# A hybrid layer's scans: adding two states' products by a transfer from GpSimd's queue, and the sum on TensorE a unit later

## The chip, the cores and the metric

One core of a Trainium2 chip runs the whole kernel as one program. The metric is the device time of one execution in microseconds. Of the core's engines, TensorE multiplies matrices into PSUM banks; VectorE, ScalarE and GpSimd work elementwise; SyncE's queue issues most of the transfers, and GpSimd can issue transfers from its own queue too. Each engine takes its instructions in the order of its own queue and waits on semaphores for the others.

## What is computed

Four blocks with residual connections run over an input of 4 sequences, 1024 tokens and 128 channels: a sparse attention, an MLP with sign weights, a Mamba block (a selective scan), and the same MLP again. The change touches the Mamba block:

```python
def step(h, inp):
    dt_t, B_t, C_t, u_t = inp
    dA = jnp.exp(dt_t[..., None] * A)
    h = dA * h + (dt_t * u_t)[..., None] * B_t[:, None, :]
    y_t = jnp.einsum('ben,bn->be', h, C_t)
    return (h, y_t)
h0 = jnp.zeros((B, E, N), x.dtype)
...
_, ys = lax.scan(step, h0, xs)
y = ys.transpose(1, 0, 2) + u2 * D_param
y = y * jax.nn.silu(z)
out = jnp.einsum('ble,ed->bld', y, W_out)
return x + res_scale * out
```

There are E = 256 channels and N = 16 states of each channel. The scan runs along the tokens, on its own for each channel and state. `y_t` is the sum over the 16 states of the state times its C.

## The kernel before

**Parts and units.** The attention runs first, up to about 242 us. Then come the first MLP and the Mamba block's preparation, and from about 312 to 866 us the scans, with the MLPs' work set between them. The scans' work is cut into eight parts, one for each of 4 sequences `b` and 2 halves `f` of its tokens (512 columns), and each part into 16 units, one for each state `n`: 128 units. A unit holds all 256 channels as two blocks `h` of 128 partitions, so that a tile `[128, 2, 512]` of float32 (512 KB) is one state of one part.

**One unit i**, by engine:

- GpSimd, `drive`: `db[i]`, the products of `dt * u` and B, one instruction of 128 x 1024, written two units ahead into one of three buffers. B comes, spread over the partitions, by a transfer `bs` of 512 KB for every two units, from SyncE's queue (`load_b`).
- ScalarE, `decay`: `da[i, h]`, the exponentials, one instruction for each block, a unit ahead.
- VectorE: two scans, one for each block, into `hs`; then one product of 128 x 1024 of `hs` with C into `hc[i]` (`hss[i]` in the code, six buffers).
- TensorE: C spread over the partitions into the one PSUM bank `pcc`, from which that product reads; and the sum over the states.

**The sum over the states.** Two states' products are first added on GpSimd (`fold`): the pair k, k + 1 (k even) is added block by block into `hc[k + 1]`, block 0 in unit k + 2 and block 1 in unit k + 3. Then TensorE (`total`) adds the pair's sum to the PSUM bank `pys` of its block, with the identity as its weights: block 0 in unit k + 3 and block 1 in unit k + 4. The first such matmul of a part comes after one with `skip_d`, which is `u2 * D_param`. After a part's last pair VectorE multiplies the gate with `pys` (`gated`), block 0 in unit k + 4 and block 1 in unit k + 5, and `mamba_out` (or `mamba_out_own` for the last four parts) multiplies it with `W_out`.

**What sets the order.** Within the scans each engine's instructions keep the order in which the program issues them. A planner sets the other work (MLP matmuls, evictions, normalisation steps, the next parts' preparation) between them: `pieces` takes pieces of it as long as the engines' clocks in `times` allow, and `spend` moves these clocks by a cost written beside each step, 1.29 for an addition of `fold`. These costs steer the order alone. The last lines of `scans` run the steps that remain after unit 127.

**The end.** After unit 127 the last pair is added and summed, the gate multiplied, and `mamba_out_own(3, 1)` and the last MLP follow in series. In TensorE's queue the rest of another MLP (tiles `pfc`, `pgc`, `pfoc`) stands between these steps.

Of the kernel before, what the change touches and what calls it, by code (L numbers as in the profile page):

```python
# [22 lines left out]
ALU = mybir.AluOpType  # L23
# [20 lines left out]
def hybrid_kernel(ctx: ExitStack, tc: tile.TileContext, x, Wq, Wk, Wv, Wo, ln_g, ln_b, W_in, conv_w,  # L44
# [17 lines left out]
    ve, te, sc, gp = (InOrder(e) for e in (nc.vector, nc.tensor, nc.scalar, nc.gpsimd))  # L62
# [1071 lines left out]
    def scans(wide, ready):  # L1134

        bss, dbs, das, hss = {}, {}, {}, {}
        py = {}
        last = len(units) - 1  # L1140

        def load_b(i):

            if i <= last and i % 2 == 0:
                b, f, n = units[i]
                ready(b, f, "b")
                bss[i] = m2.tile([P, 2, CH], F32, name=f"bs{i}", tag="bs", bufs=2)
                nc.sync.dma_start(bss[i], mamba_pre[b, f][5][n : n + 2, :].partition_broadcast(P))

        def drive(i):  # L1150
            if i <= last:
                b, f, n = units[i]
                ready(b, f, NH - 1)
                dbs[i] = m2.tile([P, NH, CH], F32, name=f"db{i}", tag="db", bufs=3)
                bs = bss[i - n % 2][:, n % 2]
                gp.tensor_tensor(dbs[i], mamba_pre[b, f][3], bs.unsqueeze(1).to_broadcast([P, NH, CH]), ALU.mult)

        def decay(i, h):
            if i <= last:
                b, f, n = units[i]  # L1160
                das[i, h] = wide.tile([P, CH], F32, name=f"da{i}_{h}", tag="da", bufs=2)
                sc.activation(das[i, h], mamba_pre[b, f][2][:, h], AF.Exp, scale=a_t[:, h, n : n + 1])

        def fold(i):

            h = i % 2
            k = i - 2 - h
            if 0 <= k <= last:
                gp.tensor_add(hss[k + 1][:, h], hss[k + 1][:, h], hss[k][:, h])

        def total(i):

            h = 1 - i % 2
            k = i - 3 - h
            if not 0 <= k <= last:
                return
            b, f, n = units[k]
            if n == 0:
                py[b, f, h] = wide.tile([P, CH], F32, name=f"pys{b}_{f}{h}", tag=f"pys{h}")
                te.matmul(py[b, f, h], skip_d[:, h], mamba_pre[b, f][1][:, h], start=True, stop=False)  # L1180
            te.matmul(py[b, f, h], ident, hss[k + 1][:, h], start=False, stop=n == N - 2)

        def gated(i):

            h = i % 2
            k = i - 4 - h
            if not 0 <= k <= last:
                return False
            b, f, n = units[k]
            if n == N - 2:  # L1190
                gate = mamba_pre[b, f][0]
                ve.tensor_mul(gate[:, h], gate[:, h], py.pop((b, f, h)))
                if h == NH - 1:
                    fed.add(("g", b, f))
            return n == N - 2


        done = {}

        def after(*keys):  # L1200
            return [done.get(k, 0.0) for k in keys]

        for i in range(3):
            load_b(i)
        for i in range(2):
            drive(i)
            done["db", i] = spend("gp", 2.38)
        for h in range(NH):
            decay(0, h)
            done["da", 0, h] = spend("sc", 0.7)  # L1210
        for i, (b, f, n) in enumerate(units):
            now[0] = i
            load_b(i + 3)
            fold(i)
            h0, h1 = i % 2, 1 - i % 2
            done["fold", i] = spend("gp", 1.29, *after(("hc", i - 1 - h0)))
            drive(i + 2)
            done["db", i + 2] = spend("gp", 2.38, *after(("hs", i - 1, 1)))
            pc = wide.tile([P, CH], F32, name=f"pcc{i}", tag="pcc")
            te.matmul(pc, spread[: 6 * N, n, :], mamba_pre[b, f][4], start=True, stop=True)  # L1220
            done["pcc", i] = spend("pe", 0.4, *after(("hc", i - 1)))
            hs = m2.tile([P, NH, CH], F32, name=f"hs{i}", tag="hs")
            db = dbs.pop(i)
            for h in range(NH):
                first = carry[b % 2][:, h, n : n + 1] if f else 0.0
                ve.tensor_tensor_scan(hs[:, h], das.pop((i, h)), db[:, h], first, ALU.mult, ALU.add)
                done["hs", i, h] = spend("ve", 1.235 if f else 1.175, *after(("da", i, h), ("db", i)))
            decay(i + 1, 0)
            done["da", i + 1, 0] = spend("sc", 0.67, *after(("hs", i, 0)))

            t = times["ve"]
            pieces(t + 2.5, lumps=False)
            if f == 0:
                sc.copy(carry[b % 2][:, :, n : n + 1], hs[:, :, CH - 1 :])
            decay(i + 1, 1)
            done["da", i + 1, 1] = spend("sc", 0.67 if f else 0.86, *after(("hs", i, 1)))
            if gated(i):
                spend("ve", 0.68, *after(("sum", i - 1)))
            hss[i] = m2.tile([P, NH, CH], F32, name=f"hc{i}", tag="hc", bufs=6)
            ve.tensor_tensor(hss[i], hs, pc.unsqueeze(1).to_broadcast([P, NH, CH]), ALU.mult)  # L1240
            done["hc", i] = spend("ve", 1.205, *after(("pcc", i)))
            total(i)
            done["sum", i] = spend("pe", 1.0, *after(("fold", i - 1)))
            t = times["ve"]
            pieces(t + 2.2)
        for i in range(last + 1, last + 6):
            fold(i)
            gated(i)
            total(i)
# [6 lines left out]
    def spend(engine, us, *others):  # L1256
        times[engine] = max(times[engine], *others, 0.0) + us
        return times[engine]
# [36 lines left out]
    def pieces(until, lumps=True):  # L1295

        forced = not until
        evictions(lumps, forced)  # L1300
        for k, rate in RATES.items():
            owed[k] = min(max(owed[k], -2 * rate) + (0 if forced else rate / 2), rate / 2)
        left = SPARE - sum(w.held for w in works)

        for w in works[:-2] + sorted(works[-2:], key=lambda w: w.count):

            moved = w in emptied and now[0] < len(units) - 10
            while w.may() and not w.next.evict and w.next.banks <= left:
                if moved and not w.next.same and not (forced and w in emptied):
                    break  # L1310
                if not (forced or w.next.hurries()):
                    if any(us and owed[k] <= 0 for k, us in w.next.us.items()):
                        break
                    if "pe" in w.next.us and ends(w)[0]["pe"] > until:
                        break
                left -= w.next.banks
                issue(w)
                moved = True
            if forced and moved:
                break  # L1320

    def ready(*part):
        while part not in prepared:
            pieces(None)
# [50 lines left out]
    with banks(SPARE), tc.tile_pool(name="wide", bufs=1, space=PSUM) as wide:  # L1375
# [21 lines left out]
        ])  # L1397
        among_scans[0] = True
        scans(wide, ready)
        among_scans[0] = False  # L1400
        works.insert(0, Work(mamba_out_own(B - 1, 1)))
# [40 lines left out]
```

## Time and profile before

| | us |
|---|---|
| median of 3 runs | 905.94 (905.73 to 910.06) |
| span of the profiled execution, first to last instruction | 901.9 |
| TensorE busy, of the span | 756.2 (84%) |
| VectorE busy | 754.3 (84%) |
| GpSimd busy | 727.0 (81%) |
| ScalarE busy | 607.1 (67%) |

The span is measured on the chip by the profiler in one execution, and the times in the first row come from runs of their own. The profile's page lists groups of instructions: engine, operation, output <- inputs, shape, count, then busy time, the mean of one in ns, the idle time just before them and what ended it. Nearly all rows name line 57, since a helper there issues every instruction; the tiles' names tell them apart. `PEld` is TensorE's loading of weights, `PE` its matmuls. A wait is put down to what came last. A row of waits reads: engine and tile, what ended the wait, us in total, times, the longest. A row of the timeline reads: start, length, engine, line, operation, tiles, shape, and in brackets the idle time before it. A table of stretches reads: from:to, length, busy us (and instructions) of each engine, the granted share of TensorE's clock, the busy share of the 16 DMA engines, and GB/s.

Two more rows for the scans, ScalarE's exponentials and VectorE's scan from a carried state:

```profile
L57 ACT ACTIVATE da<-dt,a_t 128x512 f32<-128x512 f32 x256 | 175.5, 688 | 123.2 <-DVE hs L57 122.7
L57 DVE TENSOR_TENSOR_SCAN hs<-da,carry,db 128x512 f32<-128x512 f32 x128 | 156.9, 1266 | 1.2 <-ACT da L57 1.2
```

### The profile page before, as it was taken

The numbers are of one execution on the slowest core, as the hardware profiler recorded it, in microseconds if no ns is written. First come the engines' busy times: TensorE is split into PE (matmuls) and PEld (weight loads), VectorE is DVE, ScalarE is ACT, GpSimd is POOL, SyncE is SP. The second block draws the span as 40 slices with busy tenths as digits, with TensorE's granted clock in tenths as the row PEclk, the third lists the DMA queues.
The fourth block names the chain that finished last, engine by engine and source line by source line (L and its number), as shares of the span: only waits on it lengthen the run. The fifth ranks groups of instructions, "written<-read, shape, count | busy, mean of one in ns | idle before, by whom it ended". The sixth has DMA issues, their size and how long they took to land. (4 is left out here: it accounts for less than half of the span.)

```text
span 901.9 us, 16464 instructions
## 1 busy us (share of the span) xinstructions
PE 756.2 (84%) x6226; PEld 463.5 (51%) x6226; DVE 754.3 (84%) x994; ACT 607.1 (67%) x1358; POOL 727.0 (81%) x566
## 2 busy tenths in 40 slices
PE   5897779866798978879899888779889989989777
PEld 2454546544577642335456554335455545656457
DVE  6799999999533289798899999989988898999962
ACT  4776648744445488888787888888777766654423
POOL 6799958998322199999999999999988987997930
PEclk9899989987789997789999999899989999999899
DMA  4733123330100111121221211212111121221100
GB/s 127 131 73 70 43 44 69 72 65 2 43 7 1 49 53 66 67 74 48 70 69 51 70 48 70 72 47 72 70 72 59 53 78 59 70 82 58 60 7 19
DMA packets 47152, 53.18 MB, mean 59 GB/s; under 512 B 4808, under 2 KB 38384, under 8 KB 47072
## 3 DMA queue, kind: packets, MB, share of 16 engines
q1 hardware_dynamic: 45904, 51.59, 20.4%
q8 instruction: 49, 0.80, 0.4%
q0 software_dynamic: 608, 0.27, 0.2%
q10 hardware_dynamic: 560, 0.26, 0.1%
q14 instruction: 31, 0.25, 0.1%
HBM read 45.82 MB, written 4.46 MB: 56 GB/s over the span
## 5 line engine op out<-in xcount | busy, mean ns | idle before, releaser
L57 POOL TENSOR_TENSOR db<-du,bs 128x1024 f32<-128x1024 f32 x128 | 302.4, 2363 | 0.1
L57 ACT ACTIVATE da<-dt,a_t 128x512 f32<-128x512 f32 x256 | 175.5, 688 | 123.2 <-DVE hs L57 122.7
L57 POOL TENSOR_TENSOR hc<-hc,hc 128x512 f32<-128x512 f32 x128 | 162.8, 1272 | 29.1 <-DVE hc L57 28.8
L57 DVE TENSOR_TENSOR hc<-hs,pcc 128x1024 f32<-128x1024 f32 x128 | 155.9, 1218 | 23.7 <-PE pcc L57 15.4
L57 DVE TENSOR_TENSOR_SCAN hs<-da,db 128x512 f32<-128x512 f32 x128 | 149.4, 1207 | 20.7 <-ACT da L57 15.5
L57 DVE TENSOR_TENSOR_SCAN hs<-da,carry,db 128x512 f32<-128x512 f32 x128 | 156.9, 1266 | 1.2 <-ACT da L57 1.2
L57 PE MATMUL pys<-hc,ident 128*128 128x512 f32 x256 | 145.3, 651 | 6.1 <-POOL hc L57 6.0
L57 POOL TENSOR_TENSOR prodv<-vS,E 128x128 f32<-128x128 f32 (+14 forms) x30 | 69.3, 2311 | 11.5 <-ACT E L57 11.3
L57 PEld LDWEIGHTS pys<-hc,ident 128*128 128x128 f32 x256 | 49.8, 208 | 53.7 <-issue 28.1
L57 PE MATMUL pcc<-bc,spread 96*128 96x512 bf16 x128 | 51.5, 402 | 29.6 <-DVE hc L57 28.7
L57 PE MATMUL pga<-h1a,w 128*128 128x512 f32 x256 | 70.5, 425 | 2.7 <-DVE h1a L57 1.9
L57 POOL TENSOR_TENSOR prod<-kv,qs 128x128 f32<-128x128 f32 (+14 forms) x30 | 71.1, 2369 | 0.8 <-DVE or L57 0.8
L57 ACT ACT_TABLE_LOAD x48 | 61.6, 1283 | 3.5 <-issue 2.6
L57 PE MATMUL pc<-mxnT,w_conv 128*128 128x512 f32 x128 | 61.5, 606 | 2.0 <-ACT gate L57 2.0
L57 PEld LDWEIGHTS pga<-h1a,w 128*128 128x128 f32 x256 | 49.3, 195 | 25.5 <-issue 4.7
L57 ACT ACTIVATE E<-S 128x512 f32<-128x512 f32 (+15 forms) x62 | 26.5, 473 | 39.7 <-DVE S L57 39.5
L57 PE MATMUL ps<-kx,qT 64*32 64x256 f32 x1008 | 43.5, 416 | 5.8 <-DVE S L57 5.0
L57 POOL TENSOR_TENSOR du<-dt,u 128x512 f32<-128x512 f32 x16 | 20.4, 1275 | 30.5 <-ACT dt L57 30.5
L57 ACT COPY ep<-pt 128x512 f32<-128x512 f32 x32 | 18.7, 586 | 35.8 <-DVE eo L57 35.5
L57 PEld LDWEIGHTS pc<-mxnT,w_conv 128*128 128x128 f32 x128 | 24.6, 194 | 33.9 <-issue 26.7
L57 PE MATMUL pgb<-h1b,w 128*128 128x512 f32 x128 | 37.5, 439 | 4.8 <-DVE h1b L57 3.3
L57 PE MATMUL pgc<-h1c,w 128*128 128x256 f32 (+1 forms) x192 | 37.2, 346 | 0.0
(244 smaller groups left out, 1637.5 us busy)
## 6 DMA issues: line engine op xcount, KB each, us to landing
bs<-bd SPq DMA_DIRECT2D x64, 512.0 KB
vr<-vd SPq DMA_DIRECT2D x32, 256.0 KB
vd<-kv SPq DMA_DIRECT2D x8, 256.0 KB
x<-in_L_attn_a_x_dram SPq DMA_DIRECT2D x15, 128.0 KB
kx<-kT SPq DMA_DIRECT2D x104, 16.0 KB
out_dram<-x SPq DMA_DIRECT2D x8, 128.0 KB
taps<-in_L_attn_b_conv_w_dram SPq DMA_DIRECT2D x1, 512.0 KB
out_dram<-ox SPq DMA_DIRECT2D x2, 256.0 KB
```

Source lines behind the costliest of these rows:

```text
L57: ins = getattr(self.engine, name)(*args, **kwargs)
```

## The change

`fold` no longer adds on GpSimd. For each pair GpSimd issues one transfer in SBUF that adds `hc[k]` (both blocks, 512 KB) into `hc[k + 1]`, in unit k + 2, behind that unit's `drive` where the additions stood ahead of it. `total` sums block 0 in unit k + 4 and block 1 in unit k + 5, and `gated` follows in units k + 5 and k + 6: both one unit later than before. The planner is told 0.9 for a transfer in place of 1.29 for each addition, and a sum on TensorE that depends on the transfer of two units before. The loop after the last unit is one longer.

```diff
--- before.py
+++ after.py
@@ -1163,15 +1163,16 @@
 
         def fold(i):
 
+            k = i - 2
+            if k % 2 or not 0 <= k <= last:
+                return False
+            gp.dma_start(hss[k + 1], hss[k], accum_op=ALU.add)
+            return True
+
+        def total(i):
+
             h = i % 2
-            k = i - 2 - h
-            if 0 <= k <= last:
-                gp.tensor_add(hss[k + 1][:, h], hss[k + 1][:, h], hss[k][:, h])
-
-        def total(i):
-
-            h = 1 - i % 2
-            k = i - 3 - h
+            k = i - 4 - h
             if not 0 <= k <= last:
                 return
             b, f, n = units[k]
@@ -1182,8 +1183,8 @@
 
         def gated(i):
 
-            h = i % 2
-            k = i - 4 - h
+            h = 1 - i % 2
+            k = i - 5 - h
             if not 0 <= k <= last:
                 return False
             b, f, n = units[k]
@@ -1211,11 +1212,10 @@
         for i, (b, f, n) in enumerate(units):
             now[0] = i
             load_b(i + 3)
-            fold(i)
-            h0, h1 = i % 2, 1 - i % 2
-            done["fold", i] = spend("gp", 1.29, *after(("hc", i - 1 - h0)))
             drive(i + 2)
             done["db", i + 2] = spend("gp", 2.38, *after(("hs", i - 1, 1)))
+            if fold(i):
+                done["fold", i] = spend("gp", 0.9, *after(("hc", i - 1)))
             pc = wide.tile([P, CH], F32, name=f"pcc{i}", tag="pcc")
             te.matmul(pc, spread[: 6 * N, n, :], mamba_pre[b, f][4], start=True, stop=True)
             done["pcc", i] = spend("pe", 0.4, *after(("hc", i - 1)))
@@ -1240,10 +1240,10 @@
             ve.tensor_tensor(hss[i], hs, pc.unsqueeze(1).to_broadcast([P, NH, CH]), ALU.mult)
             done["hc", i] = spend("ve", 1.205, *after(("pcc", i)))
             total(i)
-            done["sum", i] = spend("pe", 1.0, *after(("fold", i - 1)))
+            done["sum", i] = spend("pe", 1.0, *after(("fold", i - 2)))
             t = times["ve"]
             pieces(t + 2.2)
-        for i in range(last + 1, last + 6):
+        for i in range(last + 1, last + 7):
             fold(i)
             gated(i)
             total(i)
```

In the built program GpSimd's queue has 64 transfers in place of 128 additions. Its other instructions, and those of the other engines, are the same in number up to the grouping, but the planner sets them in another order. In TensorE's queue the last pair's sums now stand ahead of eight `pgc` and four `pfc` matmuls that stood ahead of them before.

## The prediction

> **What bounds the kernel now.** First the table of stretches, to see which engine is full in the stage that the change touches. It runs from the first `du` product (312 us) to the end of the last product with C (866.45); then comes the end of the program, which runs in series.
>
> ```profile
> core 0: us, PE busy (x) PEld busy (x) DVE busy (x) ACT busy (x) POOL busy (x), PEclk, DMA share, GB/s
> 312.00:866.45 554.45, 478.19 (x1731) 269.17 (x1730) 504.58 (x493) 414.49 (x876) 514.04 (x381) 0.92 0.19 64
> 866.45:869.80 3.35, 1.87 (x4) 0.78 (x5) 0.69 (x1) 0.00 (x0) 2.48 (x2) 1.00 0.00 0
> 869.80:884.05 14.25, 13.02 (x101) 10.91 (x99) 4.41 (x16) 3.98 (x11) 1.26 (x2) 1.00 0.04 10
> ```
>
> GpSimd is busy for 93% of the stage, VectorE for 91%, TensorE for 86%: 554.45 / 128 = 4.33 us a unit. Then the groups, for what one instruction costs:
>
> ```profile
> L57 POOL TENSOR_TENSOR db<-du,bs 128x1024 f32<-128x1024 f32 x128 | 302.4, 2363 | 0.1
> L57 POOL TENSOR_TENSOR hc<-hc,hc 128x512 f32<-128x512 f32 x128 | 162.8, 1272 | 29.1 <-DVE hc L57 28.8
> L57 DVE TENSOR_TENSOR hc<-hs,pcc 128x1024 f32<-128x1024 f32 x128 | 155.9, 1218 | 23.7 <-PE pcc L57 15.4
> ```
>
> A high share is not yet a bound: GpSimd runs ahead over three `db` buffers and itself waits 28.8 us for VectorE. So I asked who ended VectorE's waits in the scans, and what TensorE did before them:
>
> ```profile
> DVE hc L57 <- PE pcc L57: 15.4, 16, 2.9
> DVE hs L57 <- ACT da L57: 8.4, 14, 1.5
> ...
> DVE hs L57 <- POOL db L57: 3.0, 3, 1.6
> DVE hs L57 <- POOL hc L57: 2.1, 1, 2.1
> ```
>
> ```profile
> 360.35 0.50 PEld L57 LDWEIGHTS pys<-hc,ident 128*128 128x128 f32 x2 [1.50 <-POOL hc L57]
> ...
> 363.07 0.63 PE L57 MATMUL pcc<-bc,spread 96*128 96x512 bf16 x1
> ...
> 363.74 1.22 DVE L57 TENSOR_TENSOR hc<-hs,pcc 128x1024 f32<-128x1024 f32 x1 [1.85 <-PE pcc L57]
> ```
>
> VectorE waits for `db` for 3.0 us in all. Behind the 2.1 us put down to `hc`, ScalarE's `da` had ended only 0.1 us earlier, so I don't count it. The second fence shows the other path: TensorE's queue stands at a sum because the addition is late, so the spread C comes late and VectorE waits 1.85 us. VectorE, with other engines' small delays, sets the pace; GpSimd rarely does.
>
> **The change, part by part.**
>
> *GpSimd.* 128 additions of 1.272 us go (162.8); 64 issues come. The nearest rows are its own issues at the start:
>
> ```profile
> 247.71 0.70 POOL L869 DMA_DIRECT2D dp<-in_L_attn_b_D_param_dram  x1
> 248.40 2.12 POOL L880 DMA_DIRECT2D w_xp<-in_L_attn_b_W_xp_dram  x3
> ```
>
> ```profile
> kx<-kT POOLq DMA_DIRECT2D x8, 16.0 KB, 6.0
> w_xp<-in_L_attn_b_W_xp_dram POOLq DMA_DIRECT2D x3, 32.0 KB, 2.2
> ```
>
> I take 2.12 / 3 = 0.71, as `w_xp` also names 128 partitions; the least such row is 0.54 (`kx`), the most 1.15 (the first of the constants). So 64 x 0.71 = 45, and GpSimd falls to 514 - 163 + 45 = 396 us, 71% (70% to 77%). An issue would have to cost 162.8 / 64 = 2.54 us to give nothing back. Call T the end of the pair's second product. The issue stands behind a `db` that may start when VectorE's scan ends, T - 1.22, and ends at T + 1.14, so it finds its input ready; the `db` and layer-norm steps queued behind it wait for 0.71 us, not for data.
>
> *What VectorE gets of it.* The 3.0 us for `db`, and those `pcc` waits that come within 6 us of a sum held up by the addition: 1.85, 1.01 and 0.51 (at 363.7, 479.5 and 610.4), 3.4 together: 6.4 us. Ends: 0, if other waits take their place, and 15.4 + 3.0 + 2.1 = 20.5, if every wait for `pcc` and GpSimd goes. I take 6.4, the ones that I can follow.
>
> *The landing.* No accumulating transfer is in the trace. Nearest are GpSimd's transfers, 2.2 to 6.0 us from issue to landing, and a `bs` load of the same 512 KB:
>
> ```profile
> 561.00:563.30 2.30, 0.60 (x3) 0.21 (x2) 2.20 (x3) 2.26 (x5) 2.30 (x2) 1.00 0.61 228
> ```
>
> 228 GB/s for 2.30 us is 524 KB, the whole load. I take 2.2 + 2.3 = 4.5 us; ends 2.2 (all of it overlapped) and 6.0 + 2.3 = 8.3. TensorE reaches the sum behind `pcc` of unit k+4, whose bank is freed at T + 2 x 4.33 = T + 8.7; the issue is at T + 1.1, so 7.5 us are hidden. TensorE's idle time, (554 - 478) / 64 = 1.2 us a pair, covers up to 8.7. Cost taken: nothing; at 8.3 TensorE loses 0.8 a pair, inside its idle time. VectorE's new wait, a product written where a transfer still reads, is for a transfer three units old (13 us). The extra 33.5 MB double the DMA share of 0.19 or, with the destination read too, bring it to some 0.6. `bs` has two units, 8.7 us, for its 2.3.
>
> *One unit later.* The six `hc` buffers hold: a pair's second lives for five units, its first until the landing. The gate and what hangs on it come 4.33 us later at each part's end; other pieces fill that, except at the end. The planner, told that GpSimd is lighter, spreads the other work anew. I take nothing; half of the 15.4 us of `pcc` waits, 7 either way, is its bound.
>
> *The end, where nothing covers the landing.*
>
> ```profile
> 865.23 1.22 DVE L57 TENSOR_TENSOR hc<-hs,pcc 128x1024 f32<-128x1024 f32 x1
> ...
> 866.52 2.48 POOL L57 TENSOR_TENSOR hc<-hc,hc 128x512 f32<-128x512 f32 x2 [4.82 <-DVE hc L57]
> ...
> 867.84 2.35 PE L57 MATMUL pys<-hc,ident 128*128 128x512 f32 x4 [1.52 <-POOL hc L57]
> ```
>
> Now the sums end at 867.84 + 2.35 = 870.19. Then: issue 866.52, landed 871.0, two sums of 0.59 us, 872.2: 2.0 later. In the built order eight `pgc` (1.31 us) and four `pfc` (0.71), which stood before the last sums, come behind them: 2.0 more, on a TensorE busy 13.02 of the next 14.25 us. Together +4.0; ends 1.7 and 7.8 (landing 2.2 and 8.3).
>
> *Weighed against the Trainium skill.* DMA: Bandwidth & Descriptors (Anatomy of one DMA) gives a GpSimd transfer about 2.0 us plus bytes at 436 GB/s. By it the landing would be an estimated 3.2 us and the end 1.3 us shorter than by the rows; no run here shows it yet. SBUF — State Buffer (The "DVE blocks DMA" trap) speaks against the change: while VectorE runs a two-port instruction, GpSimd can't write descriptors. If every issue waited out a scan (1.27 us in the rows), 64 issues would take 127 us, still under 162.8, and the end would grow by 1.3; the eight `kx` issues took 0.54 to 0.81 us beside VectorE's products from PSUM, so this trace shows no such stall.
>
> **Sum.** The profiled span is 901.9; the median of the runs, 905.94, is 4.1 more, which I take as what lies around a span. 901.9 - 6.4 + 4.0 = 899.5, plus 4.1: **903.6 us**. 0.5% is 4.5 us, about what can be told from no change here: faster is under 901.4, slower over 910.5. This case's own range is 895 to 911.
>
> **Rivals.**
> - *GpSimd was the pace-setter:* all 20.5 us go: 905.9 - 20.5 + 4.0 = **889.4**. For it: 93% busy, and a `db` that never waits (0.1 us). Against: VectorE waited for `db` three times in 128 units.
> - *Hidden anyway:* the delays from GpSimd turn into waits for ScalarE or TensorE, and only the end is paid: **909.9**, up to 917 if the new order costs 7. For it: most of VectorE's waits name ScalarE or TensorE. Against: the 1.85 us above, where the addition is plainly first.
> - *TensorE is held by the landing (slower):* in TensorE's queue at the sum, in every second unit. It decides from 8.7 us on: each further us is 64. At 9.0 us: 905.9 + 0.3 x 64 + 4.0 + 4.5 (the longer end) = **933.6**. For it: an accumulation also reads its destination, which no row prices, and it meets the `bs` load. Against: both largest rows together make 8.3.
>
> **How the numbers follow.** Forecast 0.38, pace-setter 0.17, hidden anyway 0.25, held by the landing 0.20. Of the forecast 0.15 is faster, 0.21 same, 0.02 slower; the pace-setter is all faster; hidden anyway is 0.10 same and 0.15 slower; the last all slower. Faster 0.32, same 0.31, slower 0.37. The range 888 to 930 leaves out the far half of the last case and the edge of the second, some 0.15.
>
> **What would show it.** Right: GpSimd near 71% and still no wait of VectorE for `db`; issue rows of 0.7 us; the `pys` waits of TensorE for `hc` gone from the stage; the last `pys` some 5.8 us after the last product instead of 3.7. Wrong: `pys` or `pcc` waits that end with the transfer in every second unit; issue rows over 2.5 us; or VectorE over 95% busy in the stage, which would make the pace-setter right.

## The result, and the profile after

| | before | after |
|---|---|---|
| median, us | 906.46 (20 runs) | 911.53 (20 runs, 907.84 to 912.77) |
| ratio after : before | | 1.0047, 95% interval 1.0035 to 1.0060 |
| span of the profiled execution | 901.9 | 908.9 |
| first product's end to last product's end ("the scans") | 544.0 | 544.8 |
| last product's end to the span's end ("the end") | 35.5 | 41.5 |

The changed kernel is slower by 0.47%: within the 0.5% that the prediction calls no change, but the interval lies wholly on the slow side, where a gain was forecast (903.6), and 911.53 is just above the 911 where the case's own range ends. Of the 7.0 us of span 0.7 are in the scans and 6.0 in the end. What was to be won in the scans did not come.

The table of stretches, of the kernel after, with the stage up to the last product's end and then the end:

```profile
core 0: us, PE busy (x) PEld busy (x) DVE busy (x) ACT busy (x) POOL busy (x), PEclk, DMA share, GB/s
312.00:867.43 555.43, 482.07 (x1719) 267.08 (x1718) 504.28 (x493) 413.69 (x873) 416.37 (x318) 0.91 0.50 124
867.43:874.00 6.57, 1.96 (x3) 0.84 (x3) 0.00 (x1) 0.00 (x0) 0.86 (x1) 0.82 0.42 81
874.00:888.00 14.00, 14.00 (x95) 11.63 (x94) 4.64 (x16) 4.47 (x13) 1.26 (x2) 0.84 0.04 11
```

GpSimd fell from 514 to 416 us of the stage (93% to 75%), and the stage kept its length: 555.43 for 554.45. VectorE is as busy as before, 504.28. Now GpSimd's two groups, and the row of the transfers (issues, KB, median landing):

```profile
L57 POOL TENSOR_TENSOR db<-du,bs 128x1024 f32<-128x1024 f32 x128 | 305.3, 2395 | 71.6 <-DVE hs L57 37.7 <-issue 31.6 <-POOL db L57 1.8
L57 POOL DMA_DIRECT2D hc<-hc x64 | 57.7, 902 | 18.7 <-DVE hc L57 18.4
```

```profile
hc<-hc POOLq DMA_DIRECT2D x64, 512.0 KB, 4.6
```

An issue takes 0.90 us and a landing 4.6. Ahead of `db`, where GpSimd never stood idle before (0.1 us), it now does so for 71.6 us in all: GpSimd has room. VectorE's waits from 320 to 872 us show why this room brought nothing:

```profile
DVE hc L57 <- PE pcc L57: 23.6, 17, 3.4
DVE hs L57 <- ACT da L57: 15.6, 12, 8.3
DVE x L57 <- PE pfoa L57: 1.8, 2, 1.3
DVE hs L57 <- POOL rs_fb L57: 1.0, 1, 1.0
```

The waits for `db` and for the additions are gone, and those for TensorE's `pcc` have grown from 15.4 to 23.6 us. (The 8.3 in the second line is the wait of the very first scan, ahead of the first product.) Last, the chain that sets the end, in order of time (start, length, what):

```profile
866.21 1.23 DVE hc L57
867.44 0.29 issue
867.73 4.53 DMA hc<-hc
872.26 0.04 issue
872.31 3.78 PE pys L57 x4
876.09 1.71 PE pgc L57 x8
877.80 0.83 PE pfc L57 x4
```

After the last product the lone landing stands on the path for 4.53 us, and then the last two sums take 3.78 us. Each sum shows as two matmul records, and late in the scans one sum takes 1.02 us, so 3.78 is nearly twice the usual.

### The profile page after: what moved, and what is told of

Its sections match the earlier page's. It is cut to its first block, busy times and chain, and to the rows that moved or that the text cites. A ratio compares the mean times of both kernels' runs of the same rounds, so it can differ in the third digit from the quotient of the medians.

```text
span 908.9 us, 16459 instructions
## 1 busy us (share of the span) xinstructions
PE 762.8 (84%) x6226; PEld 463.4 (51%) x6226; DVE 754.0 (83%) x994; ACT 607.4 (67%) x1358; POOL 627.9 (69%) x502
## 5 line engine op out<-in xcount | busy, mean ns | idle before, releaser
L57 POOL TENSOR_TENSOR db<-du,bs 128x1024 f32<-128x1024 f32 x128 | 305.3, 2395 | 71.6 <-DVE hs L57 37.7
L57 DVE TENSOR_TENSOR hc<-hs,pcc 128x1024 f32<-128x1024 f32 x128 | 156.0, 1219 | 31.7 <-PE pcc L57 23.6
L57 PE MATMUL pys<-hc,ident 128*128 128x512 f32 x256 | 148.0, 664 | 4.6 <-DMA hc<-hc 4.6
L57 POOL DMA_DIRECT2D hc<-hc x64 | 57.7, 902 | 18.7 <-DVE hc L57 18.4
L57 ACT ACTIVATE E<-S 128x512 f32<-128x512 f32 (+15 forms) x62 | 26.5, 472 | 39.6 <-DVE S L57 39.4
```

Of the source, the lines that this page charges most:

```text
L57: ins = getattr(self.engine, name)(*args, **kwargs)
```

## The experiments

All runs, with the kernel before on the same chip beside each. The scans, the end and the waits of VectorE for `pcc` (320 to 872 us) are from one profile of each; where the first unit begins varies by 4 us between profiles whatever the kernel, so the scans are measured from product to product. A few us between two profiles are no finding by themselves: up to the last product the kernel after, D and E are the same program and show 544.8, 541.8 and 541.8, and F and K are the same and show 538.8 and 541.5. A, H and L have 6 runs each, after has 20, the others 12. The runs stand on several chips, so a comparison of two of them goes first by their ratios to before.

| run | median | ratio (interval) | scans | end | `pcc` waits |
|---|---|---|---|---|---|
| before | 906 | 1 | 544.0 | 35.5 | 15.4 |
| after | 911.53 | 1.0047 (1.0035 to 1.0060) | 544.8 | 41.5 | 23.6 |
| A, old order, nothing added | 899.95 | 0.9921 (0.9897 to 0.9946) | 539.4 | 33.8 | 12.4 |
| B, new order, nothing added | 904.59 | 0.9980 (0.9962 to 0.9997) | 543.3 | 34.0 | 21.1 |
| C, new order, GpSimd's additions | 908.70 | 1.0020 (1.0002 to 1.0039) | 544.0 | 38.2 | 21.4 |
| D, after, last pair on TensorE | 904.33 | 0.9984 (0.9965 to 1.0002) | 541.8 | 35.8 | 21.3 |
| E, after, TensorE kept busy at the end | 908.20 | 1.0027 (1.0007 to 1.0046) | 541.8 | 38.9 | 21.3 |
| F, transfer, old unit, old costs | 907.09 | 1.0009 (0.9991 to 1.0027) | 538.8 | 41.4 | 15.2 |
| G, transfer, later unit, old costs | 908.55 | 1.0033 (1.0010 to 1.0056) | 536.0 | 49.7 | 13.5 |
| H, transfer, old unit, new costs | 911.65 | 1.0053 (1.0034 to 1.0072) | 536.6 | 44.5 | 16.0 |
| I, before, last pair on TensorE | 904.66 | 0.9993 (0.9973 to 1.0013) | 544.1 | 35.0 | 15.4 |
| K, F with the last pair on TensorE | 901.95 | 0.9950 (0.9932 to 0.9968) | 541.5 | 35.1 | 15.7 |
| L, K, planner told heavier | 908.82 | 1.0045 (1.0028 to 1.0062) | 549.7 | 34.3 | 23.8 |
| M, K, planner told lighter | 905.42 | 0.9990 (0.9973 to 1.0008) | 538.0 | 39.4 | 16.9 |

### What GpSimd's relief is worth, in the old order and in the new (A, B, C)

A is the kernel before with `fold` left out; the even states are missing from its output.

```diff
             h = i % 2
             k = i - 2 - h
-            if 0 <= k <= last:
-                gp.tensor_add(hss[k + 1][:, h], hss[k + 1][:, h], hss[k][:, h])
+            return
```

> The kernel before without GpSimd's additions: TensorE sums the odd states' products alone, the even states' are left out of the sum. Every engine's order is that of before. It is the ceiling of what taking the additions off GpSimd can bring. Theory (GpSimd's additions hold nobody; VectorE and TensorE's slow stretches set the pace): the scans take the same time within 2 us, and only the end is shorter, by the 1.4 us from the last product to the first sum and some of the second addition: 903 to 905 us beside 906.5. Rival (the relief is worth what the prediction said or more, and the transfers or the new order take it back): the scans are 6.4 to 20 us shorter, 884 to 898 us.

B is the kernel after, in its order, without the transfers (the even states are missing here too):

```diff
-            gp.dma_start(hss[k + 1], hss[k], accum_op=ALU.add)
             return True
```

> The changed kernel's order, instruction for instruction, without the 64 transfers: nothing adds the even states' products, so that they are missing from the output. Theory (the new order itself costs what GpSimd's relief gives): scans of 542 to 544 us although GpSimd has neither additions nor transfers, where the same removal in the old order gave 539.4, and an end about as long as there plus the pgc and pfc behind the sums (33 us): about 905. Rival (the transfers cost the scans 5 us, by traffic, by issue time or by waits, and the order is free): scans of 539 us and about 901.

C is the kernel after, in its order, with GpSimd adding both blocks in one instruction:

```diff
-            gp.dma_start(hss[k + 1], hss[k], accum_op=ALU.add)
+            gp.tensor_add(hss[k + 1], hss[k + 1], hss[k])
```

> The changed kernel with GpSimd's addition (one instruction of 128 x 1024) in the place of each transfer: same order on every engine, same later sum, no transfers. Theory (order and lag cost nothing in the scans, the loss lies at the end where the landing stands alone): scans as before within 2 us, the end some 2.5 us shorter than the changed kernel's and TensorE less slow behind it: 906 to 909 us. Rival (the new order costs what the relief gives): with GpSimd loaded again the scans are 6 us longer or more: 914 us or more.

In the old order, taking all additions away saves 0.8%: some 7 us, of which 1.7 are in the end (35.5 to 33.8) and about 5 in the scans (544.0 to 539.4). That is the most that relief of GpSimd alone can bring there, and it lies between A's two expectations. In the new order it brings little or nothing: the scans take 544.0 us with additions, 541.8 to 544.8 in the three profiles with transfers (after, D, E) and 543.3 with neither. B and A do the same work, and B is 0.9980 - 0.9921 = 0.6%, about 5 us, slower, by its order alone (the later unit and the planner's costs together), as the theory for B had it. VectorE's waits say where. First A, then B, and then C:

```profile
DVE hs L57 <- ACT da L57: 20.4, 17, 8.3
DVE hc L57 <- PE pcc L57: 12.4, 13, 4.3
```

```profile
DVE hc L57 <- PE pcc L57: 21.1, 15, 3.9
DVE hs L57 <- ACT da L57: 16.7, 12, 8.3
```

```profile
DVE hc L57 <- PE pcc L57: 21.4, 16, 3.9
DVE hs L57 <- ACT da L57: 15.9, 11, 8.3
...
DVE hs L57 <- POOL db L57: 0.6, 1, 0.6
```

In B nothing of the change is left but the order, and VectorE still waits 21.1 us for `pcc`, 8.7 more than in A. So these waits are TensorE's own: its queue, as the planner has filled it, is late at those places. The places themselves say so too. In units 63, 85, 87 and 101 VectorE waits for `pcc` for 2.5, 2.5 to 2.6, 1.5 and 1.9 to 2.0 us in all five profiles of the new order (after, B, C, D, E), with transfers, with additions or with neither: some 8.5 us together. (Units are counted from 0.) In the five of the old order (before, A, F, I, K) it waits at none of the four. Unit 85 of the kernel after, where eight `pgb` of an MLP stand ahead of `pcc`:

```profile
683.13 1.91 PE L57 MATMUL pys<-hc,ident 128*128 128x512 f32 x2
684.06 3.94 PE L57 MATMUL pgb<-h1b,w 128*128 128x512 f32 x8
687.84 0.39 PE L57 MATMUL pcc<-bc,spread 96*128 96x512 bf16 x1
688.27 1.22 DVE L57 TENSOR_TENSOR hc<-hs,pcc 128x1024 f32<-128x1024 f32 x1 [2.53 <-PE pcc L57]
```

B also clears the transfers in the stage: the DMA share went from 0.19 to 0.50 and it cost nothing that can be seen, 543.3 us without them against 541.8 to 544.8 with them. The rest of the difference between B and after, 904.59 to 911.53, is the end: 34.0 to 41.5.

### What the end pays for (D, E, I)

D leaves the last pair out of the transfers; TensorE adds both of its products itself.

```diff
-            if k % 2 or not 0 <= k <= last:
+            if k % 2 or not 0 <= k < last - 1:
                 return False
...
+            if k == last - 1:
+                te.matmul(py[b, f, h], ident, hss[k][:, h], start=False, stop=False)
             te.matmul(py[b, f, h], ident, hss[k + 1][:, h], start=False, stop=n == N - 2)
```

> The changed kernel, but the last pair is not transferred: TensorE adds both products itself, four sums in the place of two, all else the same. Theory (nearly all of the loss is the end: the last landing alone, then TensorE at a slow clock): the last sum ends some 2 to 3 us after the last product in the place of 8.7, the matmuls behind it are at full speed again, and the time is 904 to 906 us. Rival (the loss lies in the scans): 909 us or more.

The end falls from 41.5 to 35.8, the time by 5.7 us by the ratios (1.0047 - 0.9984) and 7.2 by the medians. One pair of 64 thus cost at least what the whole change was slower by (4.3 us by the ratio).

E leaves the transfer and gives TensorE something to do while it lands:

```diff
             gated(i)
+            if i == last + 3:
+                pc = wide.tile([P, CH], F32, name="pcc_fill", tag="pcc")
+                for _ in range(4):
+                    te.matmul(pc, ident, hss[last - 2][:, 0], start=True, stop=True)
             total(i)
```

> The changed kernel with one thing added: after the last product TensorE multiplies four times a tile that it has (hc of unit 125, 128 x 512, with the identity) into the free bank pcc, which nobody reads, ahead of the last two sums. At 1.02 us each they fill 4.1 us of the 4.6 us for which TensorE stood idle at the last landing. Theory (TensorE is slow after standing idle): the last two sums, 3.78 us in the changed kernel, fall to about 2.1 and the eight pgc behind them from 2.70 to about 1.3, so the last sum ends some 7 us after the last product instead of 8.66, and the end is about 3 us shorter: about 908.5. Rival (the sums are slow because they read what has just landed, or the clock is held down for the whole stretch anyway): the sums stay at 3.8 us and the time stays within 1 us of 911.5, or grows if the four matmuls run late.

The timeline of the kernel after, from the landing on (start, length, engine, what, and in brackets the idle time before it):

```profile
867.73 0.86 POOL L57 DMA_DIRECT2D hc<-hc  x1 [6.50 <-DVE hc L57]
872.31 3.78 PE L57 MATMUL pys<-hc,ident 128*128 128x512 f32 x4 [4.61 <-DMA hc<-hc]
873.32 0.34 PEld L57 LDWEIGHTS pys<-hc,ident 128*128 128x128 f32 x1 [0.52 <-issue]
875.10 2.70 PE L57 MATMUL pgc<-h1c,w 128*128 128x256 f32 x8
```

and that of E:

```profile
864.96 3.60 PE L57 MATMUL pcc_fill<-hc,ident 128*128 128x512 f32 x8
865.05 0.86 POOL L57 DMA_DIRECT2D hc<-hc  x1 [6.50 <-DVE hc L57]
869.62 1.99 PE L57 MATMUL pys<-hc,ident 128*128 128x512 f32 x4 [1.06 <-DMA hc<-hc]
870.16 0.19 PEld L57 LDWEIGHTS pys<-hc,ident 128*128 128x128 f32 x1 [0.24 <-issue]
871.04 1.50 PE L57 MATMUL pgc<-h1c,w 128*128 128x256 f32 x8
```

The landing is as long, but behind 1.06 us of idle time the sums take 1.99 us where they took 3.78 behind 4.61, a weight load 0.19 for 0.34, and the eight `pgc` 1.50 for 2.70. The granted clock says the same, first for the kernel after and then for E, from the sums on:

```profile
872.31:878.00 5.69, 5.69 (x14) 3.63 (x15) 1.37 (x2) 0.17 (x1) 0.00 (x0) 0.50 0.00 0
869.62:874.00 4.38, 4.37 (x24) 2.94 (x24) 2.08 (x4) 0.95 (x3) 0.00 (x0) 1.00 0.00 0
```

It is 0.50 in the one and 1.00 in the other. Work that does nothing makes the end 2.6 us shorter (41.5 to 38.9), as the theory had it. The time falls by 3.3 us by the medians and 1.8 by the ratios, whose intervals overlap, so that the rows show this better than the time does. The lone landing costs twice: once as a wait, and once by leaving TensorE slow for what follows. The Trainium skill, TensorE: Matmul & The Clock Gate (HAM oscillation — how this bites in real kernels), warns of gaps of over some 3.4 us in TensorE's work, after which its clock starts again at half. These two ends agree with it, and so do F, G and H, whose last two sums take 3.78 us behind 4.91, 3.73 and 4.29 us of idle time. C shows that a shorter gap can do it: there the granted clock fell to 0.50 at 873.0, soon after 2.29 us of idle time, and the sums took 3.29 us.

I gives the kernel before D's last pair, without any transfer:

```diff
-            if 0 <= k <= last:
+            if 0 <= k < last - 1:
                 gp.tensor_add(hss[k + 1][:, h], hss[k + 1][:, h], hss[k][:, h])
...
+            if k == last - 1:
+                te.matmul(py[b, f, h], ident, hss[k][:, h], start=False, stop=False)
```

> The kernel before with its additions, but the last pair is left to TensorE, which adds both products itself. No transfer. It measures what the end owes to GpSimd's last two additions, apart from all transfers. Last sum 3.74 us after the last product in the kernel before: addition 2.48 of it. With two sums more (about 1 us each) in its place the end gains 0.5 to 1.5 us: 905 to 906, scans unchanged at 544. If it gained 4 us or more, the run with both parts would owe its gain to the end and not to GpSimd's relief.

0.9993, with an interval that holds 1: there GpSimd's additions cost the end next to nothing. The end was no problem until the transfer was put there.

### The later unit or the planner's costs (F, G, H)

F has the transfer, but all else as before: sum and gate at the old unit, and the planner told 1.29 in each unit.

```diff
-            h = i % 2
-            k = i - 2 - h
-            if 0 <= k <= last:
-                gp.tensor_add(hss[k + 1][:, h], hss[k + 1][:, h], hss[k][:, h])
+            k = i - 2
+            if k % 2 == 0 and 0 <= k <= last:
+                gp.dma_start(hss[k + 1], hss[k], accum_op=ALU.add)
...
-            fold(i)
             h0, h1 = i % 2, 1 - i % 2
             done["fold", i] = spend("gp", 1.29, *after(("hc", i - 1 - h0)))
             drive(i + 2)
+            fold(i)
```

> The kernel before with the transfers in the place of the additions, but TensorE's sum where it was, and the planner told the old costs: every engine's order is that of before. TensorE reaches the sum some 4.4 us after the pair's second product and the transfer lands 5.7 to 6 us after it. Theory: TensorE waits for the landing about 1.5 us in every second unit, most of it inside the 1.2 us that it is idle in a pair; with the end 6 us longer: 912 to 930 us, with waits of pys for the transfer in most pairs. Rival (the later sum and the new order spoil the gain): 900 us or less in the scans' favour, so a total under 906.

G adds to F the later unit alone (`total` with `k = i - 4 - h`, `gated` with `k = i - 5 - h`, as in the change):

> The changed kernel with the later unit for the sum and the gate, but the planner is told the old cost (1.29 for each addition in every unit, ahead of the db) in place of 0.9 for a transfer. It differs from the run with the transfer at the old unit, 907.09, by the later unit alone. Theory (the later unit costs the 4 to 5 us): about 911. Rival (the planner's new cost does, since it sets MLP work where TensorE is late already): about 907, with waits of VectorE for pcc of about 15 us, where the changed kernel has 23.6.

H adds to F what the planner is told alone, as the change has it:

```diff
-            done["fold", i] = spend("gp", 1.29, *after(("hc", i - 1 - h0)))
             drive(i + 2)
...
             done["db", i + 2] = spend("gp", 2.38, *after(("hs", i - 1, 1)))
+            if fold(i):
+                done["fold", i] = spend("gp", 0.9, *after(("hc", i - 1)))
...
-            done["sum", i] = spend("pe", 1.0, *after(("fold", i - 1)))
+            done["sum", i] = spend("pe", 1.0, *after(("fold", i - 2)))
```

> The changed kernel with the sum and the gate at the old unit, but with the planner told 0.9 for a transfer, behind the db, as the changed kernel tells it. It differs from the run with the transfer at the old unit, 907.09, by the planner's costs alone. Theory (the later unit costs the 4 to 5 us): about 907. Rival (the planner's new cost does): about 911, with waits of VectorE for pcc near 23 us. If both this run and the one with the later unit come out at 911, either change of the order loses the gain; if both at 907, it takes both.

| median, us | old costs | new costs |
|---|---|---|
| sum at the old unit | F 907.09 | H 911.65 |
| sum one unit later | G 908.55 | after 911.53 |

What the planner is told costs 4.6 us at the old unit by the medians (4.0 by the ratios, with intervals that lie apart). At the later unit it is 3.0 (1.3 by the ratios), and the later unit itself is 1.5 (2.2) with the old costs and nothing with the new, all with intervals that overlap. So H bears out the rival, that the costs do it, while G lies between its two expectations and leaves the later unit open. The loss is not where it was expected: in G and H the `pcc` waits are 13.5 and 16.0, the scans get shorter, 536.0 and 536.6 us, and the end longer, 49.7 and 44.5. The planner left matmuls over. The stretch after the last product, F first and then H:

```profile
861.18:902.60 41.42, 31.16 (x220) 26.74 (x220) 9.57 (x30) 9.91 (x29) 2.13 (x3) 0.91 0.11 26
```

```profile
863.17:907.70 44.53, 34.70 (x250) 29.54 (x248) 9.56 (x29) 12.07 (x35) 2.12 (x3) 0.92 0.11 24
```

220 matmul records remain in F and 250 in H (220 in the kernel before, 259 in G, where the granted clock besides stood at 0.50 from 865 to 880 us). A shorter stage is no gain where its work is only put off. F also shows that the later unit was not needed: at the old one TensorE stands waiting for a landing in the stage for 8.3 us in ten places, and the scans are as short as in A. F's own expectations, 912 or more and under 906, both missed its 907.09.

### The parts that paid, together, and how much hangs on the order (K, L, M)

K is F with D's last pair: `0 <= k < last - 1` in F's `fold`, and the added matmul in `total`.

> The order of the kernel before, the transfer for 63 pairs with its sum at the old unit, and for the last pair no transfer and no addition: TensorE adds both of its products itself, two sums more. Theory (the relief of GpSimd is worth 5 us as long as the order is kept, and the end's cost is the lone landing): scans of about 539 us and a last sum about 3.8 us after the last product, so 907.1 - 6.5 = about 900.5, some 0.6% under the kernel before. Rival (the 5 us of the run with the transfer at the old unit were chance, its time being the same as before): scans of 544 us and about 904 to 906.

901.95, some 1.5 us above what was expected and 0.5% under the kernel before: the one version that sums all the states and is clearly faster than the kernel before. Against I, which differs only in how 63 pairs are added, the transfer is worth 0.9993 - 0.9950 = 0.43%, 3.9 us.

L and M change one number in K, the cost of `fold` that the planner is told, so that no instruction of the sum changes but the order of the rest does:

```diff
-            done["fold", i] = spend("gp", 1.29, *after(("hc", i - 1 - h0)))
+            done["fold", i] = spend("gp", 1.5, *after(("hc", i - 1 - h0)))
```

with 1.5 in L and 0.9 in M.

> The run with the old order, 63 transfers and the last pair on TensorE (901.95), with one number of the planner changed: it is told 1.5 in each unit for GpSimd in place of 1.29, which moves other work (up to 667 places of TensorE's queue differ) though no instruction of the scans' sum changes. Theory A (any other order loses, since the old one was chosen among many): some 3 to 6 us slower, 905 to 908. Theory B (only telling the planner that GpSimd is lighter loses, since it then packs work too early): the same as 901.95 within 1.5 us, or faster.

> The run with the old order, 63 transfers and the last pair on TensorE (901.95), with the planner told 0.9 in each unit in place of 1.29. This order is the one of the run with the old unit and the new costs, apart from the last pair. If the loss there (911.65 against 907.09) belongs to the order, it comes back here in full: 901.95 + 4.5 = 906 to 907, with more matmuls left for after the last product. If it was the new costs together with the lone landing, 902 to 903.

By the medians L is 6.9 us slower than K and M 3.5, by the ratios 8.6 and 3.6. In L the waits for `pcc` are 23.8 us and the scans 549.7; in M the waits are 16.9, but 253 matmul records are left for the end. That is theory A, with L a little above its 905 to 908 and M a little under its 906 to 907: not that a lighter GpSimd misleads the planner, but that both other orders lose, one in the scans, the other in the end. Which of the moved pieces does it was not tried.

## Why the prediction was wrong

**The bound: right in substance.** VectorE, delayed by other engines, set the pace, and GpSimd at 93% did not. With GpSimd at 75% the stage kept its length, and in the old order A won about 5 us of the 544 by leaving all additions out.

**GpSimd: right, two terms small.** 396 us were forecast and 416.37 measured. An issue took 0.90 us, not 0.71, which is 12 us of the 20; 3 more are `db`, 305.3 us busy for 302.4, and the last 5 were not followed. All of it lies in GpSimd's idle time. No issue waited out a scan: they took 0.86 to 1.15 us beside a VectorE that was busy for 91% of the stage, so the stall that the Trainium skill, SBUF — State Buffer (The "DVE blocks DMA" trap), made thinkable did not come. The prediction's own evidence on this does not hold, though: its eight `kx` issues ran from 24.30 to 28.90 us, most of them while VectorE stood idle, in the 4.52 us up to 29.79, and not beside its products.

**What VectorE gets: 6.4 us, nearly half of it misread.** The 3.0 for `db` were real: in F, with the old order, that wait is gone. Of the 3.4 for `pcc` only 0.51 were. The profile of before put 1.50 us of idle time at a sum's weight load down to `POOL hc`, and I took the addition for the cause. But the idle time is that of the weight load alone: TensorE's matmuls `pd` ran up to 360.42, past the load's start at 360.35:

```profile
358.51 1.91 PE L57 MATMUL pd<-dtl,w_dt 8*128 8x512 f32 x2
```

F keeps the order of before and has no addition, and it shows the same 1.50 us, with no releaser named, and the same wait of VectorE:

```profile
360.99 0.50 PEld L57 LDWEIGHTS pys<-hc,ident 128*128 128x128 f32 x2 [1.50 <-issue]
...
364.38 1.22 DVE L57 TENSOR_TENSOR hc<-hs,pcc 128x1024 f32<-128x1024 f32 x1 [1.85 <-PE pcc L57]
```

The second wait, 1.01 us, is 1.02 in F and 1.01 in A; the third, 0.51, is gone in both. In the kernel after there is no addition either, and the rows of the first stand there with nearly the same numbers:

```profile
361.27 0.50 PEld L57 LDWEIGHTS pys<-hc,ident 128*128 128x128 f32 x2 [1.50 <-issue]
361.27 2.08 PE L57 MATMUL pys<-hc,ident 128*128 128x512 f32 x2
...
364.00 0.63 PE L57 MATMUL pcc<-bc,spread 96*128 96x512 bf16 x1
...
364.67 1.22 DVE L57 TENSOR_TENSOR hc<-hs,pcc 128x1024 f32<-128x1024 f32 x1 [1.86 <-PE pcc L57]
```

TensorE ran slowly there: 2.08 us for two records that take 1.02 late in the scans, and 0.63 for a `pcc` that takes 0.38 there, with a granted clock of 0.50 from that sum to VectorE's product in before, after, A and F alike. The addition had merely ended at about the time at which the queue got to it. The relief was nevertheless worth 3.9 to 5 us in the old order (K against I, A against before), near the 6.4 of the forecast, but the reason given for nearly half of it does not hold. In A the waits that fell are 3.0 us for `db`, the 2.1 for `hc` that the prediction did not count, and 3.0 for `pcc`, most of them at other places, while those for `da` grew by 3.7 (without the first scan's).

**The order: taken at nothing. This step failed.** "The planner, told that GpSimd is lighter, spreads the other work anew. I take nothing" turned out to be 3 to 5 us by the ratios: B against A 5.3, D against K 3.1 (the same 63 transfers and the last pair on TensorE in both; their intervals just touch), H against F 4.0, M against K 3.6. In the changed kernel it shows as 8.2 us more waits for `pcc` (5.9 in D and E), with 8.5 at the four places that only its order has, and it used up the relief of GpSimd: D against I, with ends alike, gains 0.09%, with intervals that overlap. The bound of 7 either way held it. The middle of that bound was the wrong choice: all three other orders whose price was measured by itself (H, L, M) lose against the one that stood there, L even by 8.6. Three are few, but they speak for a likely loss and not for an even chance.

**The landing: right in size, right to be hidden in the scans.** 4.5 us forecast, 4.6 measured. That the sum of a small transfer's 2.2 us and a load's 2.3 came so near may be luck, as no run splits the landing. In the stage of the changed kernel no wait of TensorE ends with a transfer. By the Trainium skill, DMA: Bandwidth & Descriptors (Anatomy of one DMA), it would have been an estimated 3.2 us; the row was nearer.

**The end: +4.0 forecast, +6.0 measured.** The landing began 0.3 us after the last product and not at once. The last two sums were priced at two times 0.59 us, the time of one record, though each sum is two, and E shows 1.99 for both at the full clock; behind the idle time they took 3.78. These put the last `pys` 8.66 us after the last product (867.43 to 876.09), where 5.8 were forecast and 3.74 stood before: +4.9 for a term of 2.0. The other term, 2.0 for `pgc` and `pfc` behind the sums, measured next to nothing: F has them ahead of the sums and an end of 41.4, after has them behind and 41.5. From the last `pys` to the end of the span both take 32.8 us and before takes 31.7, so F has the last 1.1 of the +6.0 without that term.

**Together.** Forecast were -6.4 for the relief and +4.0 for the end. The runs give -4 to -5 for the relief, +3 to +5 for the order and +6.0 for the end: +4 to +7, where 4.3 (by the ratio) to 5.1 (by the medians) were measured.

**The rivals.** "Hidden anyway" was the nearest: 909.9 with an end of 4.0, or 911.9 with the measured 6.0, against 911.53. It was given 0.25 for the right observation, that most of VectorE's waits named TensorE or ScalarE. That its number fits so well is in part luck: it took the relief to be worth nothing, where the old order shows 4 to 5 us that the new order happened to cancel. The pace-setter fell with A: without any addition 899.95, 10 us above its 889.4, which held an end that A does not even pay. TensorE held by the landing fell in the kernel after, which shows no such wait in the stage, and F shows 8.3 us of them that cost the scans nothing.

## What to carry to other kernels

Before counting a wait as a gain, look whether the instruction named as its releaser is the cause: measure the waiting engine's own instructions there, and run the same order without the releaser; here TensorE ran at half speed, and the wait stayed. Where a planner's costs set the order, an edit that corrects a cost is an edit of the whole order; test it by itself, and count the work left over after the stage together with the stage. And a transfer that is free while a stage runs is paid in full, and again in TensorE's speed, where it stands alone at the end: here it paid to give the last pair to TensorE, which stood idle.

## What the runs showed of the hardware

An accumulating transfer of 512 KB in SBUF from GpSimd's queue took 0.90 us to issue and 4.6 us to land (median of 64, 4.5 to 6.7), and 4.53 us at the end, where VectorE stood idle: VectorE's work did not lengthen it much. Sixty-four of them raised the DMA share from 0.19 to 0.50 without slowing VectorE (504.28 us busy, 504.58 before) and hardly `db` on GpSimd (2395 ns for 2363).

TensorE came out of 4.61 us of idle time at about half its speed (granted clock 0.50, a weight load 0.34 us for 0.19) and stayed there through two sums and eight more matmuls, up to about 878 us; behind 1.06 us of idle time it did not (granted clock 1.00). In C it fell to 0.50 soon after 2.29 us of idle time.
